# Graph network layer: the nodes' gates as tanh of the sums in PSUM, gated and added to the residual by three instructions per tile

## The chip, the cores and the metric

The kernel runs on one core of a Trainium2 chip. The time is the device time of one execution in microseconds (us), lower is better. Engines are named as in the profile: PE is TensorE, DVE is VectorE, ACT is ScalarE, POOL is GpSimd, and SP is the engine whose queue starts most transfers.

## The reference

One layer of a graph network with 12500 nodes and 400000 edges, the edges sorted by destination, all in float32, and then a residual and a layer norm. A node has 160 features: 64 scalars `s` and 32 vectors `v` of three components; `a` is the node's attribute. Cut to what matters:

```python
h_s = s @ lin1_ws * a / sqrt(64);  h_v = einsum('nci,cd->ndi', v, lin1_wv) * a / sqrt(32)
w1, w2, w3, w4, w5 = split(silu(edge_scalars @ fc_w1 / sqrt(64)) @ fc_w2 / sqrt(64))
es, ev = h_s[edge_src], h_v[edge_src]
mid_s, mid_v = products of w1..w5, es, ev and the four edge attributes
agg = segment_sum(mid, edge_dst) / 4
o_s = agg_s @ lin2_ws * a / sqrt(96);  o_v = agg_v @ lin2_wv * a / sqrt(128)
pre_s = s @ sc_ws * a / sqrt(64) + o_s          # 96 columns
pre_v = v @ sc_wv * a / sqrt(32) + o_v          # 32 x 3
scalars = silu(pre_s[:, :64]);  gates = sigmoid(pre_s[:, 64:96])
out = layernorm(x + concat(scalars, gates * pre_v))
```

Both `silu(z) = z * sigmoid(z)` and the gating of the vectors are a product with `sigmoid(z)` of the 96 columns of `pre_s`.

## The kernel before

**Start.** The table `h_tab` of 12500 rows of 160 numbers (`h_s`, `h_v`) is computed from the nodes and written to HBM; the destinations are turned into positions `rel` inside blocks of edges (L398, L403).

**The loop over edges.** 400000 edges are 3125 tiles of 128. A step takes four tiles; there are 782 steps. In a step:

- POOL issues four indirect transfers, `gather` (L452): each fetches the 128 rows of `h_tab` that a tile's sources name, into one of four buffers `hg`. POOL does nothing else in the loop.
- PE multiplies the hidden layer by `fc_w2` into `pw` (L465, PSUM, two buffers). The hidden layer itself comes every second step (`hidden`: PE L443, ACT silu L445).
- DVE makes the one-hot matrix of the destinations in a free part of `pw` (L528, from `rel` and `iota`, both in SBUF), the products of `pw` and `hg` (L475 and three times L483, one operand in PSUM and one in SBUF), and the selection matrix `sel` (L537, from the one-hot in PSUM).
- PE sums the products by destination into `pa` (L544), two steps later.

Every two blocks of three tiles, ACT copies `pa` to SBUF (L740), PE transposes it (L553), ACT copies that (L556, L558); for up to sixteen blocks together PE applies `lin2` (L568), ACT copies the result to `os` (L571), and DVE adds each block to the window of `acc` that begins at the block's first node (L576, all in SBUF). `acc` holds the sums of all nodes in SBUF, 96 rows (columns of `pre_s`, and of `pre_v`) by node. The self connection is added to it piece by piece (L720, L721).

**The nodes, inside the same loop.** When no later block can touch a group of four node tiles any more, `begin` takes up its job, one stage in each step (25 groups; `finish` issues the load of `xt`, the rows of x, at that moment in program order). In the stage `turn(k)`, one tile a step, PE transposes two 96 x 128 pieces of `acc` into a PSUM bank of the pool `misc` (two banks, shared with L443, L553, L568 and L720), and DVE multiplies by the attribute into `z`, in SBUF (L604). The multiplication stands between L475 and the first L483 of that step. The other stages stand at the end of a step, after `sel` and the additions to `acc`: `gates` (ACT sigmoid, L610), `gated` (DVE L615 and L616, two for each tile), `residual` (DVE L624, one for each tile), `moments` (L629, L631), `root` (ACT, L635) and `norm` (L639, L641, and the transfer to the output, L644). So a group of four takes ten steps. The last group of four tiles is done behind the loop; there each of L615, L616 and L624 takes all four tiles at once (`spans`).

**The order.** Within the loop the instructions of PE, DVE, ACT and POOL are issued in program order. The order of SP's queue, which starts the loads of `es`, `idx`, `eat`, `xt` and the output, is made by a planner. ACT loads a table (ACT_TABLE_LOAD) where a function is not in the table set that is loaded; the build places these.

Of the kernel before, what the change touches and what calls it, by code (L numbers as in the profile page):

```python
# [10 lines left out]
F32 = mybir.dt.float32  # L11
# [3 lines left out]
AF = mybir.ActivationFunctionType  # L15
OP = mybir.AluOpType
# [4 lines left out]
P = 128  # L21
S = 64
V = 32
V3 = 3 * V
D = S + V3
# [28 lines left out]
def gnn_kernel(  # L54
# [21 lines left out]
    nc = tc.nc  # L76
    N = x.shape[0]
    NT = attr.shape[1]
# [8 lines left out]
    consts = ctx.enter_context(tc.tile_pool(name="consts", bufs=1))  # L87
# [100 lines left out]
    def load_chunk(c, queue=nc.sync):  # L188
        if c in ess:
            return  # L190
        t0, halves = chunks[c]
        es = ess[c] = loads.tile([2 * S, SIDE * P], F32, name="es")
        for half, n in enumerate(halves):
            to = es[half * S:(half + 1) * S]
            e0 = (t0 + half * halves[0]) * P
            queue.dma_start(to[:, :n * P], es_t[:, e0:e0 + n * P])


    ident = consts.tile([P, P], F32, name="ident")
# [24 lines left out]
    with tc.tile_pool(name="nodes", bufs=len(starts)) as nodes, tc.tile_pool(  # L224
        name="nodes_ps", bufs=6, space=PSUM
# [22 lines left out]
        at = consts.tile([P, NT], F32, name="at")  # L248
# [60 lines left out]
        for c0, cn, quarters, cq, xa, xz in loaded:  # L309
# [3 lines left out]
            nt = -(-cn // P)  # L313
            first = c0 // P
            full = cn // P
            for t0 in range(0, nt, U):
# [5 lines left out]
                k = min(U, full - t0)  # L322
# [32 lines left out]

    load_chunk(0, nc.gpsimd)
    nc.gpsimd.dma_start(dt, dst)
    iota = consts.tile([P, W], F32, name="iota")
    nc.vector.tensor_copy(iota, iota_i)
    for half in range(2):  # L360
# [22 lines left out]
    for to, part, pieces, w, r0, c0, by in maps:  # L383
        for k, piece in enumerate(pieces):
# [3 lines left out]
            m = terms.setdefault((to, part, four), len(terms))  # L388
# [20 lines left out]
    acc = sums.tile([V3, 2, NP], F32, name="acc")  # L409
# [169 lines left out]
    def finish(fin, psum, t0, nt, p, most=NF):  # L579


        whole = nt if p == P else nt - 1
        spans = [(0, nt)] if t0 + nt == tiles_of_nodes else [(k, k + 1) for k in range(nt)]
        xt = fin.tile([P, most, D], F32, name="xt", bufs=2)
        held = []
        if whole < nt:
            nc.vector.memset(xt[:, whole], 0.0)
        parts = [(slice(t0 * P, (t0 + whole) * P), slice(0, whole), P)] if whole else []
        if whole < nt:
            parts.append((slice((t0 + whole) * P, (t0 + whole) * P + p), slice(whole, nt), p))  # L590
        for nodes_of, k, n in parts:
            nc.sync.dma_start(xt[:n, k], x[nodes_of, :].rearrange("(t p) d -> p t d", p=n))

        def turn(k):
            if not held:
                held.extend(fin.tile([P, most, *shape], F32, name=name) for name, shape in (
                    ("z", [2 * V3]), ("sg", [V3]), ("y", [D]), ("st", [6]), ("mv", [2]),
                    ("rs", [])))
            z = held[0]
            c = (t0 + k) * P  # L600
            pp = psum.tile([P, 2, V3], F32, name="pp", tag="misc")
            for m in range(2):
                nc.tensor.transpose(pp[:, m], acc[:, m, c:c + P], ident[:V3, :V3])  # L603
            return lambda: nc.vector.tensor_scalar(  # L604
                z[:, k], pp.rearrange("p m c -> p (m c)"), at[:, t0 + k:t0 + k + 1], None,
                op0=OP.mult)

        def gates():
            z, sg = held[:2]
            nc.scalar.activation(sg[:, :nt], z[:, :nt, :V3], AF.Sigmoid)  # L610

        def gated():
            z, sg, y = held[:3]
            for k, m in spans:
                nc.vector.tensor_mul(y[:, k:m, :S], z[:, k:m, :S], sg[:, k:m, :S])  # L615
                nc.vector.tensor_mul(  # L616
                    y[:, k:m, S:].rearrange("p t (c i) -> p t i c", i=3),
                    z[:, k:m, V3:].rearrange("p t (i c) -> p t i c", i=3),
                    sg[:, k:m, None, S:].to_broadcast([P, m - k, 3, V]))

        def residual():
            y = held[2]
            for k, m in spans:
                nc.vector.tensor_add(y[:, k:m], y[:, k:m], xt[:, k:m])  # L624

        def moments():
            _, _, y, st, mv, _ = held
            for k in range(nt):
                nc.vector.bn_stats(st[:, k], y[:, k])  # L629
            for k in range(nt):  # L630
                nc.vector.bn_aggr(mv[:, k], st[:, k])  # L631

        def root():
            mv, rs = held[4:]
            nc.scalar.activation(rs[:, :nt], mv[:, :nt, 1], AF.Sqrt, bias=eps)  # L635

        def norm():
            _, _, y, _, mv, rs = held
            nc.vector.reciprocal(rs[:, :nt], rs[:, :nt])  # L639
            for k in range(nt):  # L640
                nc.vector.tensor_scalar(y[:, k], y[:, k], mv[:, k, 0:1], rs[:, k:k + 1],  # L641
                                        op0=OP.subtract, op1=OP.mult)
            for nodes_of, k, n in parts:
                nc.sync.dma_start(out[nodes_of, :].rearrange("(t p) d -> p t d", p=n), y[:n, k])  # L644

        return [lambda k=k: turn(k) for k in range(nt)] + [
            gates, gated, residual, moments, root, norm]


    tiles_of_nodes = -(-N // P)  # L650
# [5 lines left out]
    with tc.tile_pool(  # L656
        name="fin", bufs=1
    ) as fin, tc.tile_pool(
        name="late", bufs=2
    ) as late, tc.tile_pool(name="edge", bufs=2) as edge, tc.tile_pool(  # L660
        name="deep", bufs=4
# [140 lines left out]
        def begin():  # L802

            if to_do and not turning and not doing:
                t, nt, p = to_do[0]
                end = (t + nt - 1) * P + p
                if not waiting or min(waiting) * RATE >= end + MARGIN:
                    job = finish(fin, misc_ps, *to_do.pop(0))
                    turning.extend(job[:nt])
                    doing.extend(job[nt:])  # L810

        with tc.manual_schedule(engines={ENG.PE, ENG.DVE, ENG.Activation, ENG.Pool}):
# [6 lines left out]
            for n, (c, i, tiles) in enumerate(steps):  # L819
# [36 lines left out]
                if n % 30 == 13 and pieces:  # L856
                    products_due.extend([lambda: (lambda: None)] * 3 + self_connection(pieces.pop(0)))
            assert not pieces and not products_due
            last_steps = finish(fin, misc_ps, *last_job, most=LAST)
            n = len(steps)  # L860
            while waits:
# [28 lines left out]
        with tc.For_i(0, n_redo, 1):  # L890
# [9 lines left out]
            with tc.For_i(0, n_again, 1) as g, tc.For_i(0, GT, 1) as k:  # L900
                t = g * GT + k
# [12 lines left out]
                for k, op in enumerate((OP.min, OP.max)):  # L914
# [14 lines left out]
                                        op1=OP.mult)  # L929
# [17 lines left out]
            for pool, job, most in [(fin, job, NF) for job in jobs] + [(fin, last_job, LAST)]:  # L947
                job_steps = finish(pool, misc_ps, *job, most=most)
                for f in job_steps[:job[1]]:
                    f()()  # L950
                for f in job_steps[job[1]:]:
                    f()
# [46 lines left out]
```

## Time and profile before

| | us |
|---|---|
| median of three runs | 4023.07 (4021.55 to 4029.47) |
| the profiled execution, its own time | 4018.78 |
| its span in the profile | 4017.0 |
| ACT's table loads at L445, L610, L635 | 61.6, 32.1, 32.1 (48, 25 and 25 of them) |
| ACT's activations at L610 | 12.6 and 0.4 (24 and 1) |
| idle time of PE before L603, of it for L604 | 90.7, 15.7 |

A line of a group in the profile reads: line, engine, operation, output <- inputs, shapes, count | busy us in all, mean ns of one | idle time of the engine before it, and what ended it. A line of the timeline reads: start, duration, engine, line, operation, count, and in brackets the idle time before it. Consecutive instructions of one line are merged there ("x4"), and the recorded ends of two instructions on DVE can overlap a little.

### The profile page before, as it was taken

The numbers are of one execution on the slowest core, as the hardware profiler recorded it, in microseconds if no ns is written. First come the engines' busy times: TensorE is split into PE (matmuls) and PEld (weight loads), VectorE is DVE, ScalarE is ACT, GpSimd is POOL, SyncE is SP. The second block draws the span as 40 slices with busy tenths as digits, with TensorE's granted clock in tenths as the row PEclk, the third lists the DMA queues.
The fourth block names the chain that finished last, engine by engine and source line by source line (L and its number), as shares of the span: only waits on it lengthen the run. The fifth ranks groups of instructions, "written<-read, shape, count | busy, mean of one in ns | idle before, by whom it ended". The sixth has DMA issues, their size and how long they took to land. (4 is left out here: it accounts for less than half of the span.)

```text
span 4017.0 us, 46675 instructions
## 1 busy us (share of the span) xinstructions
PE 3676.3 (92%) x14291; PEld 1588.0 (40%) x14291; DVE 2410.5 (60%) x6596; ACT 938.7 (23%) x2463; POOL 2982.9 (74%) x3144
## 2 busy tenths in 40 slices
PE   6899899999999999999999999999899989999997
PEld 4344343343343433334333443344343334333443
DVE  5556565655655655656656655666565665655655
ACT  2222222221222222212212222222121221222222
POOL 4777777777777777777777777777777777777775
PEclk8999999999999999999999999999999999999999
DMA  8444444443444444444444444444444444444442
GB/s 240 95 100 98 98 104 96 103 106 94 101 102 98 103 98 102 103 100 101 101 99 100 95 106 101 96 106 99 98 105 95 105 102 95 103 101 98 100 96 58
DMA packets 227691, 411.71 MB, mean 102 GB/s; under 512 B 71883, under 2 KB 157383, under 8 KB 226535
## 3 DMA queue, kind: packets, MB, share of 16 engines
q0 software_dynamic: 152272, 266.53, 27.9%
q1 hardware_dynamic: 74646, 142.01, 14.7%
q8 instruction: 115, 1.88, 0.2%
q14 instruction: 144, 1.18, 0.1%
q10 hardware_dynamic: 514, 0.10, 0.0%
HBM read 392.41 MB, written 16.00 MB: 102 GB/s over the span
## 5 line engine op out<-in xcount | busy, mean ns | idle before, releaser
L452 POOL DMA_INDIRECT hg<-h_tab,idx x3125 | 2968.7, 950 | 962.2 <-issue 865.5
L465 PE MATMUL pw<-w,hid 128*128 128x448 f32 x3126 | 1376.5, 564 | 191.5 <-DVE sel L537 150.1
L544 PE MATMUL pa<-pr,sel 128*64 128x416 f32 x6250 | 1303.5, 539 | 0.0
L475 DVE TENSOR_TENSOR pr<-pw,hg 128x512 f32<-128x512 f32 x782 | 540.5, 691 | 1042.4 <-DMA hg<-h_tab,idx 784.2
L483 DVE TENSOR_TENSOR pr<-pw,hg 128x384 f32<-128x384 f32 x2346 | 1153.6, 547 | 0.0
L465 PEld LDWEIGHTS pw<-w,hid 128*128 128x128 f32 x3126 | 556.3, 195 | 685.8 <-issue 445.3
L544 PEld LDWEIGHTS pa<-pr,sel 128*64 128x64 f32 x6250 | 388.0, 139 | 812.3 <-issue 799.4
L740 ACT COPY sa<-pa 128x416 f32<-128x416 f32 x521 | 263.1, 505 | 1415.4 <-PE pa L544 1413.0
L443 PE MATMUL misc<-es,w 128*128 128x512 f32 (+1 forms) x784 | 448.0, 654 | 17.0 <-DMA es<-in_es_t_dram 14.3
L528 DVE TENSOR_TENSOR pw<-rel,iota 128x64 f32<-128x64 int16 x782 | 178.4, 228 | 468.3 <-PE pw L465 465.5
L445 ACT ACTIVATE hid<-misc 128x512 f32<-128x512 f32 x392 | 233.5, 596 | 743.9 <-PE misc L443 743.4
L553 PEld LDWEIGHTS misc<-ident,sa 128*128 128x128 f32 x2084 | 239.6, 141 | 311.6 <-issue 252.1
L568 PE MATMUL misc<-tt,l 128*96 128x256 f32 (+5 forms) x1496 | 346.0, 378 | 1.7 <-ACT tt L558 1.5
L553 PE MATMUL misc<-ident,sa 128*128 128x128 f32 x2084 | 328.1, 280 | 0.9 <-DVE acc L721 0.8
L537 DVE TENSOR_TENSOR sel<-pw,eas 128x256 f32<-128x256 f32 x782 | 323.6, 414 | 0.0
L556 ACT COPY tt<-misc 128x192 f32<-128x192 f32 x521 | 164.5, 316 | 517.2 <-PE misc L553 516.7
L568 PEld LDWEIGHTS misc<-tt,l 128*96 128x96 f32 (+1 forms) x1496 | 227.0, 162 | 139.6 <-issue 72.6
L443 PEld LDWEIGHTS misc<-es,w 128*128 128x128 f32 x784 | 119.2, 191 | 283.2 <-issue 228.5
L576 DVE TENSOR_TENSOR acc<-acc,os 96x32 f32 x1042 | 195.6, 188 | 23.9 <-ACT os L571 5.5
L603 PE MATMUL misc<-ident,acc 96*128 96x96 f32 x196 | 36.4, 272 | 90.7 <-DVE pw L528 41.8
L558 ACT COPY tt<-misc 128x64 f32<-128x64 f32 x521 | 117.1, 225 | 0.0
L571 ACT COPY os<-misc 96x512 f32<-96x512 f32 (+2 forms) x68 | 38.3, 563 | 303.1 <-PE misc L568 280.4
(84 smaller groups left out, 653.0 us busy)
## 6 DMA issues: line engine op xcount, KB each, us to landing
es<-in_es_t_dram SPq DMA_DIRECT2D x258, 384.0 KB
hg<-h_tab,idx POOLq DMA_INDIRECT x3125
h_tab<-ht POOLq DMA_DIRECT2D x6, 1280.0 KB
xt<-in_x_dram SPq DMA_DIRECT2D x23, 320.0 KB
out_dram<-y SPq DMA_DIRECT2D x23, 320.0 KB
xv<-in_xv_t_dram SPq DMA_DIRECT2D x25, 187.5 KB
xs<-in_xs_t_dram SPq DMA_DIRECT2D x25, 125.0 KB
xa<-in_xs_t_dram SPq DMA_DIRECT2D x6, 512.0 KB
```

The lines of the kernel that those rows point to most:

```text
L443: nc.tensor.matmul(ph[:k, c], w1[:k, :k], es[:k, t0 * P + c0 * P:t0 * P + c1 * P], start=True, stop=True)
L445: nc.scalar.activation(hid[:k, c], ph[:k, c], AF.Silu, scale=1.0 / math.sqrt(64))
L452: nc.gpsimd.indirect_dma_start(out=hg[:, t, :], out_offset=None, in_=h_tab, in_offset=bass.IndirectOffsetOnAxis(ap=i, axis=0))
L465: nc.tensor.matmul(pw[:, t:t + m, :NWT], hid[:m * S, c * P:(c + 1) * P], w2[:m * S, :m], start=True, stop=True)
L475: nc.vector.tensor_mul(two, pw[:, :n, :2 * S].rearrange("p t (k c) -> p t k c", k=2), hg[:, :n, None, :S].to_broadcast([P, n, 2, S]))
L483: nc.vector.tensor_mul(pr[:, :n, first:first + V3].rearrange("p t (i c) -> p t i c", i=3), pw[:, :n, None, 2 * S + k * V:2 * S + (k + 1) * ...
L537: nc.vector.tensor_mul(sel[:, :n], oh[:, :, None, :].to_broadcast([P, n, 4, W]), by_slot(tiles[0][0])[:, u:u + n, :, None].to_broadcast([P ...
L544: nc.tensor.matmul(pa[half * ROWS:(half + 1) * ROWS, :NPR], sel[:, t].rearrange("p k w -> p (k w)"), pr, start=start, stop=stop)
L553: nc.tensor.transpose(pt[:, four * P:four * P + k], sa[:k, c:c + P], ident[:k, :k])
L568: nc.tensor.matmul(po[:, k, :nb], l2[r, terms[to, part, four]], a[:, :nb], start=(n == 0), stop=(n == len(of) - 1))
L576: nc.vector.tensor_add(window, window, os[:, :, b])
L740: nc.scalar.copy(sa, pas.pop(j)[:, :NPR])
```

## The change

The gate is written with `sigmoid(a*p) = (1 + tanh(a*p/2)) / 2`, p being the sums before the multiplication by the attribute. `half_at` is half of the attribute, made once ahead of the loop. In `turn(k)` ACT takes the tanh straight from the PSUM bank, with `half_at` as its scale, into `g` in SBUF. Then DVE, at the place where L604 stood, issues three instructions for the tile: `(g + 1) * p` for the scalars and for the vectors, both read from and written to the same PSUM bank, and `that * half_at + xt` into `y`. The stages `gates`, `gated` and `residual`, the tile `z`, and the batching of the last group fall away; a group of four takes seven steps.

```diff
+    half_at = consts.tile([P, NT], F32, name="half_at")
+    nc.vector.tensor_scalar_mul(half_at, at, 0.5)
...
-        spans = [(0, nt)] if t0 + nt == tiles_of_nodes else [(k, k + 1) for k in range(nt)]
...
-            z = held[0]
+            g, y = held[:2]
             c = (t0 + k) * P
-            pp = psum.tile([P, 2, V3], F32, name="pp", tag="misc")
+            pp = psum.tile([P, 512], F32, name="pp", tag="misc")
             for m in range(2):
-                nc.tensor.transpose(pp[:, m], acc[:, m, c:c + P], ident[:V3, :V3])
-            return lambda: nc.vector.tensor_scalar(
-                z[:, k], pp.rearrange("p m c -> p (m c)"), at[:, t0 + k:t0 + k + 1], None,
-                op0=OP.mult)
-
-        def gates():
-            z, sg = held[:2]
-            nc.scalar.activation(sg[:, :nt], z[:, :nt, :V3], AF.Sigmoid)
-
-        def gated():
-            z, sg, y = held[:3]
-            for k, m in spans:
-                nc.vector.tensor_mul(y[:, k:m, :S], z[:, k:m, :S], sg[:, k:m, :S])
-                nc.vector.tensor_mul(
-                    y[:, k:m, S:].rearrange("p t (c i) -> p t i c", i=3),
-                    z[:, k:m, V3:].rearrange("p t (i c) -> p t i c", i=3),
-                    sg[:, k:m, None, S:].to_broadcast([P, m - k, 3, V]))
-
-        def residual():
-            y = held[2]
-            for k, m in spans:
-                nc.vector.tensor_add(y[:, k:m], y[:, k:m], xt[:, k:m])
+                nc.tensor.transpose(pp[:, m * V3:(m + 1) * V3], acc[:, m, c:c + P], ident[:V3, :V3])
+            half = half_at[:, t0 + k:t0 + k + 1]
+            nc.scalar.activation(g[:, k], pp[:, :V3], AF.Tanh, scale=half)
+            pg = pp[:, 2 * V3:2 * V3 + D]
+
+            def gate():
+                nc.vector.scalar_tensor_tensor(pg[:, :S], g[:, k, :S], 1.0, pp[:, :S],
+                                               op0=OP.add, op1=OP.mult)
+                nc.vector.scalar_tensor_tensor(
+                    pg[:, S:].rearrange("p (c i) -> p i c", i=3),
+                    g[:, k, None, S:].to_broadcast([P, 3, V]), 1.0,
+                    pp[:, V3:2 * V3].rearrange("p (i c) -> p i c", i=3),
+                    op0=OP.add, op1=OP.mult)
+                nc.vector.scalar_tensor_tensor(y[:, k], pg, half, xt[:, k],
+                                               op0=OP.mult, op1=OP.add)
+
+            return gate
...
         return [lambda k=k: turn(k) for k in range(nt)] + [
-            gates, gated, residual, moments, root, norm]
+            moments, root, norm]
```

More of the change, by code (lines that the diff above doesn't have):

```diff
@@ L596, in turn @@
                 held.extend(fin.tile([P, most, *shape], F32, name=name) for name, shape in (
-                    ("z", [2 * V3]), ("sg", [V3]), ("y", [D]), ("st", [6]), ("mv", [2]),
-                    ("rs", [])))
-            z = held[0]
+                    ("g", [V3]), ("y", [D]), ("st", [6]), ("mv", [2]), ("rs", [])))
+            g, y = held[:2]
             c = (t0 + k) * P
-            pp = psum.tile([P, 2, V3], F32, name="pp", tag="misc")
+            pp = psum.tile([P, 512], F32, name="pp", tag="misc")
@@ L626, in moments @@
+            return gate
         def moments():
-            _, _, y, st, mv, _ = held
+            _, y, st, mv, _ = held
             for k in range(nt):
@@ L633, in root @@
         def root():
-            mv, rs = held[4:]
+            mv, rs = held[3:]
             nc.scalar.activation(rs[:, :nt], mv[:, :nt, 1], AF.Sqrt, bias=eps)
         def norm():
-            _, _, y, _, mv, rs = held
+            _, y, _, mv, rs = held
             nc.vector.reciprocal(rs[:, :nt], rs[:, :nt])
```

## The prediction

> **What bounds the kernel now.** I began with the page's busy times.
>
> ```profile
> span 4017.0 us, 46675 instructions
> PE 3676.3 (92%) x14291; PEld 1588.0 (40%) x14291; DVE 2410.5 (60%) x6596; ACT 938.7 (23%) x2463; POOL 2982.9 (74%) x3144
> ```
>
> TensorE looks like the bound, GpSimd does not. So I asked next, of each engine, what it waited for. This is GpSimd's answer (total us, times, longest):
>
> ```profile
> POOL hg L452 <- issue: 865.5, 2841, 0.3
> POOL hg L452 <- DVE pw L528: 22.8, 75, 0.3
> POOL hg L452 <- DMA h_tab<-ht: 10.5, 1, 10.5
> ```
>
> After the first gather, no wait of GpSimd is longer than 0.3 us, whatever is named: that is the fixed gap between two gathers. The view of the gathers' tile has their durations:
>
> ```profile
> L452 POOL DMA_INDIRECT hg<-h_tab,idx x3125: 942/946/2035, 65.4 to 3984.9; - x196
> ```
>
> A gather (0.946) and its gap (0.30) make 1.250 us, and 3124 x 1.25 = 3905.0 of the 3919.4 us between first and last start. The loop is one unbroken chain of gathers on GpSimd, and its length is 3905.0 plus what single gathers lose. TensorE and VectorE follow it: VectorE waits 784.2 us in all for gathered rows. They would hold it up only by freeing one of the four hg buffers late. From the last product of a step (L483) to the first gather that reuses its buffer there were 11.0 us in the median, 4.8 at the least (step 4), 5.7 after step 30. No delay below that can reach the end.
>
> So the question is what makes single gathers slow: 14.4 us in all. I laid GpSimd's timeline beside VectorE's. GpSimd around the second longest gather:
>
> ```profile
> 2463.54 0.94 POOL L452 DMA_INDIRECT hg<-h_tab,idx  x1 [0.30 <-issue]
> 2464.79 1.97 POOL L452 DMA_INDIRECT hg<-h_tab,idx  x1 [0.30 <-issue]
> 2467.07 0.95 POOL L452 DMA_INDIRECT hg<-h_tab,idx  x1 [0.30 <-issue]
> ```
>
> VectorE at that moment:
>
> ```profile
> 2464.47 0.40 DVE L576 TENSOR_TENSOR acc<-acc,os 96x32 f32 x2
> 2464.79 1.02 DVE L624 TENSOR_TENSOR y<-y,xt 128x160 f32<-128x160 f32 x4
> 2465.73 0.22 DVE L528 TENSOR_TENSOR pw<-rel,iota 128x64 f32<-128x64 int16 x1
> ```
>
> The gather starts as the four residual additions start and ends 1.02 us late: exactly their length. Going through all 3125 starts, the time above 1.250 sums to 5.5 us over the 47 intervals in which the gating products L615 or L616 ran, 5.6 us over the 45 with L624, 1.0 over 5 at the start (L398, L403), 0.9 over 548 with the additions L576, 0.5 over 442 with the one-hot L528, and 0.1 over the 1958 intervals beside all else, L475, L483, L537 and L604 among them. (The missing 0.6 is 3124 x 0.0002, the median's own fraction.) The dividing line is where the operands are: L615, L616, L624, L576, L528 and L398 read two tensors from SBUF. L483 and L537 read one from PSUM and one from SBUF, and cost the gathers nothing. When a run of the first kind covers a gather's start, the gather ends later by about what is left of that run.
>
> **The change, part by part.** The rows that price it:
>
> ```profile
> L483 DVE TENSOR_TENSOR pr<-pw,hg 128x384 f32<-128x384 f32 x2346 | 1153.6, 547 | 0.0
> L604 DVE TENSOR_SCALAR z<-misc,at 128x192 f32<-128x192 f32 x98 | 39.8, 408 | 0.4 <-PE misc L603 0.4
> L641 DVE TENSOR_SCALAR y<-y,mv,rs 128x160 f32<-128x160 f32 x98 | 30.7, 373 | 0.9
> L616 DVE TENSOR_TENSOR y<-z,sg 128x96 f32<-128x96 f32 (+1 forms) x95 | 27.2, 286 | 0.0
> L624 DVE TENSOR_TENSOR y<-y,xt 128x160 f32<-128x160 f32 (+1 forms) x95 | 24.9, 321 | 0.0
> L615 DVE TENSOR_TENSOR y<-z,sg 128x64 f32<-128x64 f32 (+1 forms) x95 | 20.6, 217 | 0.6 <-ACT sg L610 0.6
> ```
>
> Removed on VectorE: 39.8 + 27.2 + 24.9 + 20.6 = 112.5 us. Added: 98 times three scalar_tensor_tensor, a form the trace lacks. At 1.04 ns an element, L483 is 400 + 147 ns, L641 167 + 206 with pointer scalars. So I estimate 64 elements at 0.22, 96 at 0.26 and 160 with a pointer at 0.37 us: 0.85 a tile, 83 us. VectorE's 29 us less lie beside the gathers and are worth nothing by themselves. On ScalarE 25 sigmoids (12.6 + 0.4) go, with the 25 table loads at L610 (32.1) and some 25 reloads for silu. 98 tanh come: the sigmoid takes 523 ns for 384 elements and 364 for 192, so 0.28 for 96. That too is beside the gathers.
>
> The trace shows no tanh. The built program's order puts no table load before a tanh in the loop; sqrt keeps its pair. The Trainium skill (ScalarE: Activation LUTs, Table sets: the hidden batching unit) speaks against mixing functions, lists tanh with exp and with sigmoid, and silu nowhere in that table. By it each turning step would pay a load for tanh and one for silu, and with the 1283 ns that a load takes here VectorE would start a gate 1.3 us later: still inside the 5.7, so the sum would be the same.
>
> What acts on the chain: the 11.2 us (5.5 + 5.6, unrounded 11.16) lost to L615, L616 and L624 go, if the new three cost the gathers nothing. The first two read g from SBUF and the sums from PSUM, the third PSUM, xt and a pointer. Bounds: nothing, by the 1958 intervals; or what two SBUF operands cost. For that I laid a run of 0.82 us from each start of z (L604) over the gathers' starts: it covers 75 and sums to 32.3 us. I take nothing: L483 has the same places of operands as the third, L604 a pointer, and both are in the free group. The Trainium skill (GPSIMD Engine Reference, Key points) names VectorE instructions with two SBUF inputs, as seen here, but also those in a 2-port mode; were L641, SBUF to SBUF with one tensor, such a one, it would be a loss that this change leaves in place. The 46 intervals beside L641 lost 0.1 us.
>
> What moves: in a turning step the gate occupies VectorE for some 0.82 us where z took 0.32 (start to start), so the additions and the next one-hot come 0.5 us later against the gathers. Only 41 turning steps have such additions. Shifting them in the trace by 0.35 to 0.65 us makes them cover 7 to 18 starts, 0.3 to 0.7 us. I take +0.6; bounds -0.9 (all that L576 costs now) to 41 x 0.12 (its largest single loss) = +4.9.
>
> New waits. A gate waits for its tanh, and L483 and the selection queue behind it on VectorE. ScalarE is 23% busy and what stands before the tanh is matched to earlier matmuls, so this is a fraction of a microsecond against 5.7. The PSUM bank of the turned sums is held about 0.5 us longer; TensorE waited 15.7 us for z, may wait some 50 more, and has 340 us of idle time. Three steps fewer per group end the job earlier. SP's queue: xt needs the buffer of two groups before, and is issued when that group's residual ends (2465.83, behind the L624 above), a whole group ahead of its use, so reading it at the first turn waits for nothing; in the built order xt moves ahead of one pair of es loads, whose buffer comes free eight steps of 5.0 us before use. half_at is one instruction of 0.2 us before the gathers.
>
> The tail, from the last sums to the statistics:
>
> ```profile
> 4001.06 0.63 DVE L641 TENSOR_SCALAR y<-y,mv,rs 128x160 f32<-128x160 f32 x2
> 4001.63 0.74 DVE L604 TENSOR_SCALAR z<-misc,at 128x192 f32<-128x192 f32 x2
> 4002.72 0.74 DVE L604 TENSOR_SCALAR z<-misc,at 128x192 f32<-128x192 f32 x2 [0.35 <-PE misc L603]
> 4005.09 0.82 DVE L624 TENSOR_TENSOR y<-y,xt 128x640 f32<-128x640 f32 x1
> 4005.95 1.01 DVE L629 BATCH_NORM_STATS2 st<-y 128x6 f32<-128x160 f32 x4
> ```
>
> The group before ends in the loop after the change, so its L641 is gone here. First pair turned by 4001.5, tanh 4001.8, then four gates of 0.82 to 0.90 us, the third behind its bank: 4005.3 where L629 began at 4005.95. I take -0.65; bounds -2 to +1.
>
> Sum: 4018.78 - 11.2 + 0.6 - 0.65 = 4007.5 by the profiled execution. That one is 4.3 us under the median of the runs (4023.07; 4021.55 to 4029.47), so the same step gives 4011.8. Part of that scatter may itself be such losses and would go too: 4011.5.
>
> **The rivals.**
> Losses move (17%): the later additions and one-hots land on starts much oftener than the shift says. For: each gather start is a target every 1.25 us. Against: 41 steps, at most 0.12 us each in the trace. Price 4.9, or 11.8 if all 98 tiles paid: 4016 to 4023.
> The chain does not react (7%): the long gathers have another cause in those steps, such as SP's xt transfer. For: it is issued in the same step. Against: at 2464.79 the gather is already running when xt goes out. Only the tail is left: 4022.4.
> Slower (8%): the three PSUM instructions hold GpSimd off as two SBUF operands do. Place: the gate run in each turning step; price 32.3 - 11.2 - 0.65 = +20.4, so 4043.5. It decides from 11.85 / 98 = 0.12 us per tile. Against: L483 and L604.
>
> **How the numbers follow.** The forecast has 68%. 0.2% (8.05 us, about what a measurement of this kernel can tell) is passed in most of it: 0.65 faster, with a little of the first rival. Within: 0.27. Slower: 0.08. The range: 4005 (bounds -0.9 and -2, and no offset between profile and median) to 4022, which takes in +4.9 and +1 with the offset and most of the rivals within 0.2%; the slow rival is left out.
>
> **What would show it.** Right: no gather interval above 1.4 us in the node steps, first to last gather start some 10.5 us under 3919.4, and L629 at the end 20.5 us after the last gather's start (21.1 now). Wrong: gathers still long where VectorE runs the gate; a GpSimd wait over 0.3 us (a buffer freed late); table loads beside tanh; VectorE waiting for xt.

## The result and the profile after

| | before | after |
|---|---|---|
| median us (runs, lowest to highest) | 4024.39 (10, 4019.44 to 4033.12) | 4014.72 (10, 4006.09 to 4017.3) |
| after / before | | 0.9971, 95% interval 0.9963 to 0.998 |
| the profiled execution, its own time | 4018.78 | 4006.09 |
| first to last gather start, from the timeline | 3919.43 | 3909.84 |
| of it above 3124 x 1.250 | 14.4 | 4.8 |

The change makes the kernel 9.7 us faster: 0.24%, by the interval 0.2 to 0.37%. From the page of the profile after, GpSimd's waits and the view of the gathers' tile, these are the lines that stand against those of before:

```profile
span 4004.3 us, 46674 instructions
PE 3666.2 (92%) x14291; PEld 1586.3 (40%) x14291; DVE 2407.4 (60%) x6508; ACT 897.4 (22%) x2488; POOL 2973.4 (74%) x3144
...
POOL hg L454 <- issue: 848.3, 2785, 0.3
...
POOL hg L454 <- DMA h_tab<-ht: 6.6, 1, 6.6
...
L454 POOL DMA_INDIRECT hg<-h_tab,idx x3125: 942/946/1278, 61.3 to 3971.1; - x196
```

The gathers' median is 946 ns as before, the longest 1278 ns where it was 2035 (after: L454, at the start of the loop; before: L452). VectorE is busy for 3 us less and ScalarE for 41 less; both lie beside the chain of gathers, which accounts for the time. The two profiled executions differ by 12.7 us, and the differences come from three places:

- The chain of gathers, 9.6 us: 3919.43 - 3909.84.
- The first gather, 4.15 us: it starts at 61.27 where it was 65.42, since GpSimd waited 6.6 us for the last write of the table and not 10.5. That is not the change's doing. In the other profiles on chips of this speed it started between 61.7 and 64.4 us. It may be one source of the runs' scatter.
- The end, -1.0 us: from the last gather's start to the end of the span it takes 33.2 us where it took 32.15.

The chain's 9.6 us are also what the medians moved by (9.67); that the two agree to 0.1 us is chance, since the medians' own interval is 8.0 to 14.9 us. The timeline shows a gate with a gather in it, VectorE and GpSimd together:

```profile
2287.47 0.23 DVE L609 SCALAR_TENSOR_TENSOR misc<-g,misc 128x64 f32<-128x64 f32 x1
2287.73 0.26 DVE L611 SCALAR_TENSOR_TENSOR misc<-g,misc 128x96 f32<-128x96 f32 x1
2288.03 0.38 DVE L616 SCALAR_TENSOR_TENSOR y<-misc,half_at,xt 128x160 f32<-128x160 f32 x1
2288.15 0.94 POOL L454 DMA_INDIRECT hg<-h_tab,idx  x1 [0.30 <-issue]
```

The gather starts 0.12 us into the addition of xt and takes 0.94 us, the normal time. Over all 169 intervals in which L609, L611 or L616 ran, the time above 1.250 sums to -0.02 us, and none is over 0.03. What is left of the loss is 2.5 us beside the additions (now L578), 0.7 beside the one-hot (now L530), 1.0 at the start (L400, L405) and 0.3 in the 51 intervals with L636, the last multiplication of a tile (L641 before, where it was 0.1 in 46).

### The profile page after: what moved, and what is told of

Read it like the earlier page. It is cut to its first block, busy times and chain, and to the rows that moved or that the text cites. A ratio compares the mean times of both kernels' runs of the same rounds, so it can differ in the third digit from the quotient of the medians.

```text
span 4004.3 us, 46674 instructions
## 1 busy us (share of the span) xinstructions
PE 3666.2 (92%) x14291; PEld 1586.3 (40%) x14291; DVE 2407.4 (60%) x6508; ACT 897.4 (22%) x2488; POOL 2973.4 (74%) x3144
## 5 line engine op out<-in xcount | busy, mean ns | idle before, releaser
L454 POOL DMA_INDIRECT hg<-h_tab,idx x3125 | 2959.2, 947 | 958.2 <-issue 848.3
L485 DVE TENSOR_TENSOR pr<-pw,hg 128x384 f32<-128x384 f32 x2346 | 1152.6, 546 | 0.0
L530 DVE TENSOR_TENSOR pw<-rel,iota 128x64 f32<-128x64 int16 x782 | 178.6, 228 | 500.6 <-PE pw L467 498.8
L578 DVE TENSOR_TENSOR acc<-acc,os 96x32 f32 x1042 | 195.2, 187 | 25.2 <-ACT os L573 6.9
```

Of the source, the lines that this page charges most:

```text
L454: nc.gpsimd.indirect_dma_start(out=hg[:, t, :], out_offset=None, in_=h_tab, in_offset=bass.IndirectOffsetOnAxis(ap=i, axis=0))
L485: nc.vector.tensor_mul(pr[:, :n, first:first + V3].rearrange("p t (i c) -> p t i c", i=3), pw[:, :n, None, 2 * S + k * V:2 * S + (k + 1) * ...
L578: nc.vector.tensor_add(window, window, os[:, :, b])
```

## The experiments

The theory: GpSimd's gather is delayed when it starts while VectorE reads two tensors from SBUF, and the change helps because its three instructions read one of them from PSUM. The rivals: it helps because four tiles' instructions in a row became one tile's three at a time; or because sigmoid and its table loads went; or the losses had another cause in those steps.

The first four ran on a chip on which the kernel before took 4019.69 us (median of 28) and GpSimd's chain was the bound as in the profile of before. "Loss" is the time above 1.250 us between two gather starts, put down to the VectorE line that ran in that interval.

**All operands in SBUF, the instructions where the change has them.** ScalarE copies the sums to SBUF and the intermediate stays in SBUF; the rest is the changed kernel:

```diff
+            nc.scalar.copy(zs[:, k], pp[:, :2 * V3])
-            pg = pp[:, 2 * V3:2 * V3 + D]
+            pg = us[:, k]
...
-                ... g[:, k, :S], 1.0, pp[:, :S] ...
+                ... g[:, k, :S], 1.0, zs[:, k, :S] ...
-                    pp[:, V3:2 * V3].rearrange("p (i c) -> p i c", i=3),
+                    zs[:, k, V3:].rearrange("p (i c) -> p i c", i=3),
```

> The changed kernel with the same stages, places and instruction counts on VectorE, but the gate's operands in SBUF: ScalarE copies the turned sums to SBUF behind the tanh, and the three scalar_tensor_tensor read and write SBUF only. Theory (two SBUF operands hold the gathers off): laying a run of 0.85 us from each first gate instruction of the changed kernel's trace over its gather starts covers 70 starts and sums to 30.5 us; a gather may slip in between two of the three, so 10 to 30 us are lost there: the chain of gathers 3920 to 3940 us instead of 3909.8, and a time 10 to 30 us over the changed kernel's. Rival (the dense burst of eight or four instructions in one step is what hurts, and the change spread it over four steps): no loss, 3909 to 3911, the changed kernel's time.

Measured: 4007.97 us, ratio to before 0.9971 (0.9959 to 0.9982); chain 3915.75. The gate's lines (L612, L614, L619) lost 1.36 us in 169 intervals, the longest 0.14. The theory asked for 10 to 30 us: its size was wrong by about a factor of ten. The timeline shows why:

```profile
3258.40 0.21 DVE L612 SCALAR_TENSOR_TENSOR us<-g,zs 128x64 f32<-128x64 f32 x1
3258.53 0.28 DVE L614 SCALAR_TENSOR_TENSOR us<-g,zs 128x96 f32<-128x96 f32 x1
3258.85 0.38 DVE L619 SCALAR_TENSOR_TENSOR y<-us,half_at,xt 128x160 f32<-128x160 f32 x1
3258.97 1.08 POOL L454 DMA_INDIRECT hg<-h_tab,idx  x1 [0.30 <-issue]
```

The same phase as in the example above, 0.12 us into the addition of xt, and with both operands in SBUF the gather is 0.14 us late. So the place of the operands does decide. But the delay ends 0.26 us after that instruction's start (starts at 0.17 and 0.22 lose 0.09 and 0.04), and the gathers that start 0.13 to 0.39 us after the start of L614 lose 0.01 us at most: they get through before L619, which waits for L614's result. The gate is not one run of 0.82 us but short ones with openings, and little is lost even from SBUF. This run's other 9.4 us of loss lie beside the additions (2.65), the one-hot (1.36), the start (1.2), and 4.2 over all other intervals. Of the 4.2, 0.52 is a single wait of GpSimd for L485 (0.82 us in the place of 0.30, at 3547 us). Most of the rest is no delay of single gathers: all through this run the undisturbed gathers took 1 to 3 ns longer (median 947 ns, many at 949), which makes some 3 us in these intervals. Why is open. The profiled execution was the longest of the kernel's seven (4012.13 us), so its chain need not be that of the median.

**The addition of xt alone reading two tensors from SBUF.**

```diff
-            pg = pp[:, 2 * V3:2 * V3 + D]
+            pg = us[:, k]
```

> The changed kernel, only the product of the first two gate instructions written to SBUF instead of PSUM, so that the third reads two tensors from SBUF and the first two still one from PSUM. Theory: only the third holds gathers off; a run of 0.2 to 0.28 us from its places in the changed kernel's trace covers 12 to 14 starts and sums to 1.8 to 2.9 us: chain 3911 to 3913. Rival (dense burst): 3909 to 3911. Either is within 0.2% of the changed kernel; the gathers that start during the third instruction tell them apart.

Measured: 4010.94 us, 0.9976 (0.9967 to 0.9985); chain 3910.88. The addition (L618 there) lost 0.83 us over 118 intervals, the longest 0.14, with the same phases: starts 0.12 to 0.18 us into it lose 0.14 to 0.09. By its size alone the chain would fit the rival as well; it is the phases that tell for the theory, since in the changed kernel starts at the same places lose nothing (0.83 us in all was lost where the theory had 1.8 to 2.9).

**The old stages, with tanh.** The kernel before with its stages, buffers and places, `half_at` and tanh in the place of sigmoid, `(g + 1) * z` in the place of `z * sg`:

```diff
-            nc.scalar.activation(sg[:, :nt], z[:, :nt, :V3], AF.Sigmoid)
+            nc.scalar.activation(sg[:, :nt], z[:, :nt, :V3], AF.Tanh)
...
-                nc.vector.tensor_mul(y[:, k:m, :S], z[:, k:m, :S], sg[:, k:m, :S])
+                nc.vector.scalar_tensor_tensor(y[:, k:m, :S], sg[:, k:m, :S], 1.0, z[:, k:m, :S],
+                                               op0=OP.add, op1=OP.mult)
```

> The kernel before with one part of the change alone: tanh in place of the sigmoid (half of the attribute in the first multiplication, and 1 + tanh in the two gating products), all in SBUF and in the old stages. Some 50 of ScalarE's 98 table loads go. Theory: time as before within 0.2%, gathers still lose 8 to 14 us beside the gating products and the residual. Rival (the table loads or the tanh brought the gain): the changed kernel's time, about 0.3% below.

Measured: 4016.99 us, 0.9997 (0.9988 to 1.0006); chain 3919.56. ScalarE is busy for 876.1 us where it was 938.7, with the table loads beside the gate gone but one, and the losses are what they were: 5.1 us at the gating, 6.0 at the residual. Tanh and fewer table loads bring nothing by themselves. In the changed kernel, tanh has no load beside it either.

**The additions ahead of the selection.** After the change, half of the remaining loss lies beside the additions L578. Here they stand before `sel`, whose first operand is in PSUM, so that they are no longer followed by the next step's one-hot:

```diff
-                sel = select_quad(edge, tiles, oh)
                 for a in ready:
                     add(*a)
+                sel = select_quad(edge, tiles, oh)
```

> The changed kernel with the additions to the nodes' sums moved ahead of the selection matrix, so that they no longer end where the next one-hot begins (both read two tensors from SBUF). Theory: the 2.5 us lost beside additions in the changed kernel fall to 0.5 to 2, as a run of 0.4 us that no longer joins the one-hot; chain 3908 to 3910, time the same within 0.2%. If additions lose more at their new phase, up to 41 x 0.2 = 8 us more.

Measured: 4008.86 us, 0.9973 (0.9964 to 0.9982); chain 3910.63. The loss did not go, it changed its name: 0.55 us beside the additions (the longest 0.03) and 2.24 beside the one-hot (the longest 0.15). So it is the one-hot (228 ns), and not the additions (187 ns each), that delays gathers here, though both read two tensors from SBUF. The changed kernel's timeline shows it, once one looks for it:

```profile
1820.08 0.41 DVE L578 TENSOR_TENSOR acc<-acc,os 96x32 f32 x2
1820.35 1.09 POOL L454 DMA_INDIRECT hg<-h_tab,idx  x1 [0.30 <-issue]
1820.40 0.22 DVE L530 TENSOR_TENSOR pw<-rel,iota 128x64 f32<-128x64 int16 x1
```

The gather starts late in the additions, the one-hot 0.05 us after the gather, and the gather is 0.14 us late. A VectorE instruction can still delay a gather that has started just before it.

**The operands' place by itself.** The other kernels ran on chips where the kernel before took 5089 to 5189 us: there, with a granted clock of 0.87 to 0.88 where it was 0.97, GpSimd waits for VectorE, so the time of a kernel says little about the gathers and the gathers' own durations are compared. What sets this is open. GpSimd's largest wait in the first of these kernels:

```profile
POOL hg L454 <- DVE pr L485: 1020.8, 229, 11.9
```

The measure is the duration of a gather above 0.946 us, summed over those gathers in whose first 0.3 us the line in question ran. By it, the gates and residuals of the kernel before lose 5.52 us (28 gathers) + 5.62 (24) = 11.1 us, as by the starts. Sums of this measure are taken from the trace's nanoseconds; the timeline's two decimals are too coarse for sums over hundreds of gathers.

Three kernels add one VectorE instruction of 128 x 320 elements to every step of the changed kernel, its result unused: the sum of two SBUF tensors, the sum of one tensor in PSUM and one in SBUF, and one SBUF tensor times a constant.

```diff
+                sc = edge.tile([P, Q, 80], F32, name="sc")
+                nc.vector.tensor_add(sc[:, :m], one, two)               # both in SBUF
+                nc.vector.tensor_add(sc[:, :m], pw[:, :m, :80], two)    # or: one in PSUM
+                nc.vector.tensor_scalar_mul(sc[:, :m], one, 2.0)        # or: one tensor, in SBUF
```

> The changed kernel with one more addition on VectorE at the end of each of the 782 steps, 128 x 320, both operands in SBUF, into a scratch tile that nobody reads. Theory: laying a run of 0.35 us at that place over the gather starts of the changed kernel covers 176 starts and sums to 34 us, some more where the next one-hot joins it: time 25 to 70 us over the changed kernel's. Rival (VectorE's busy time, whatever the operands): the same as with one operand in PSUM.

> The same extra addition at the same place, one operand in PSUM (the step's own pw) and one in SBUF. Theory: 0 to 4 us over the changed kernel, though VectorE has 782 x 0.48 = 375 us more to do: the gathers' chain does not see it. Rival (VectorE's busy time): as with two SBUF operands.

> The same place and size, a multiplication by a constant with its one tensor in SBUF. By the trace of before, where 46 gather intervals beside L641 lost 0.1 us, 0 to 4 us over the changed kernel. By the rule of the Trainium skill (GPSIMD Engine Reference, Key points) that an instruction in a 2-port mode contends as well, a loss like that with two SBUF operands, shorter by the time the mode saves: 10 to 40 us.

The first two were run again on another chip:

> The changed kernel with one more addition on VectorE at the end of each of the 782 steps, 128 x 320, both operands in SBUF. On the chip where it ran first the kernel before itself took 5089 us and GpSimd waited for VectorE, so the times said nothing; the gathers' own busy time was 53 us above that with one operand in PSUM. On a chip where the gathers are the chain: 30 to 70 us over the changed kernel's time. Rival (VectorE's busy time, whatever the operands): the same as with one operand in PSUM.

> The same extra addition, one operand in PSUM: 0 to 4 us over the changed kernel, though VectorE has 374 us more to do. Rival: as with two SBUF operands.

| the added instruction | its mean ns | gathers beside it | they lose, us | longest | ratio of times (95%) |
|---|---|---|---|---|---|
| SBUF + SBUF | 489 | 461 | 52.1 | 0.56 | 1.0013 (0.9981 to 1.0046) |
| again | | 447 | 48.2 | 0.54 | 0.9948 (0.9916 to 0.998) |
| PSUM + SBUF | 478 | 446 | -0.24 | 0.03 | 1.0103 (1.0072 to 1.0134) |
| again | | 449 | 0.05 | 0.13 | 1.0032 (0.9998 to 1.0066) |
| one SBUF tensor | 334 | 358 | 11.2 | 0.24 | 1.0018 (0.9983 to 1.0052) |

The pair differs in the place of one operand, and with it the loss comes and goes, some 110 ns for each gather against nothing. Two thirds of it lie in the 137 gathers that also had the additions L578 just ahead of the added one (34 of the 52 us); with the operand in PSUM the 133 gathers at that place lose nothing. What was expected of the times could not be read there, and no run shows this loss in a kernel's time: the kernel with no delayed gathers was even the slower of the two. One example from the timeline of each, SBUF and SBUF:

```profile
116.19 0.48 DVE L844 TENSOR_TENSOR sc<-w,l 128x320 f32<-128x320 f32 x1
116.27 1.23 POOL L454 DMA_INDIRECT hg<-h_tab,idx  x1 [0.30 <-issue]
```

PSUM and SBUF:

```profile
226.24 0.48 DVE L844 TENSOR_TENSOR sc<-pw,l 128x320 f32<-128x320 f32 x1
226.31 0.95 POOL L454 DMA_INDIRECT hg<-h_tab,idx  x1 [0.30 <-issue]
```

One SBUF tensor:

```profile
2998.16 0.32 DVE L844 TENSOR_SCALAR sc<-w 128x320 f32<-128x320 f32 x1
2998.24 1.05 POOL L454 DMA_INDIRECT hg<-h_tab,idx  x1 [0.30 <-issue]
```

Each gather starts 0.07 or 0.08 us into the instruction; they take 0.28, 0.00 and 0.10 us longer than 0.946. The third is the surprise: one SBUF tensor is enough in this form. It is not the one-hot that follows: 282 of the 358 gathers have none beside them, and these lose 7.9 us of the 11.2. (About 1 us of the 11.2 is no delay: in this run the median gather takes 949 ns and not 946.) So of the two expectations the trace's 0 to 4 us failed, and the skill's 10 to 40 us held, at its lower edge and in gather time. In the first kernel, the gathers with no one-hot near lose 0.27 us in the mean where they start 0.05 to 0.15 us into the addition, 0.14 at 0.2, 0.065 at 0.3 and nothing from 0.35 on: the delay ends some 0.14 us before the instruction's recorded end.

**The old bursts, one operand of each in PSUM.** The counterpart of the first experiment: stages, order and bursts of the kernel before, but the gating and the residual read columns of `pw` in the place of the gate and of `y`. The gate and the gated sums are so left out of what is computed.

```diff
-                nc.vector.tensor_mul(y[:, k:m, :S], z[:, k:m, :S], sg[:, k:m, :S])
+                nc.vector.tensor_mul(y[:, k:m, :S], z[:, k:m, :S], now["pw"][:, k:m, :S])
...
-                nc.vector.tensor_add(y[:, k:m], y[:, k:m], xt[:, k:m])
+                nc.vector.tensor_add(y[:, k:m], now["pw"][:, k:m, :D], xt[:, k:m])
```

> The kernel before with its stages and bursts as they were (eight gating products, then four additions, back to back at the end of a step), but the sigmoid operand of the products, and y in the residual, replaced by columns of the step's own pw in PSUM: the gate and the first operand of the residual are left out of the computation. All twelve instructions then read one tensor from PSUM. Theory (a run of instructions with two SBUF operands holds a gather until the run ends): the 11.2 us go although the bursts stay; chain 3908 to 3911 us, time about 0.25 to 0.3% below the kernel before. Rival (the burst itself hurts, which would explain why the gate in SBUF at one tile a step lost only some 1.4 us): the chain stays at 3918 to 3921 and the time as before.

Measured: 5185.29 us where before took 5176.7 there, 1.0009 (0.9986 to 1.0032); the expected chain and time could not be read on this chip, where GpSimd waits 1182.8 us for L483. The 31 gathers beside the gating lose 0.00 us and the 23 beside the residual 0.03, in the place of 5.52 (28 gathers) and 5.62 (24). In the timeline a gather starts in the middle of the four residual additions and is not late:

```profile
915.66 1.01 DVE L626 TENSOR_TENSOR y<-pw,xt 128x160 f32<-128x160 f32 x4
915.92 0.94 POOL L452 DMA_INDIRECT hg<-h_tab,idx  x1 [0.30 <-issue]
```

With it the four corners are filled, in us of gather time lost at the gates and residuals, by durations:

| | both operands in SBUF | one in PSUM |
|---|---|---|
| in bursts of up to four tiles | 11.1 (before) | 0.0 |
| a tile at a time | 1.1 (all in SBUF) | 0.0 (after) |

Either half of the change alone takes away nine tenths of the loss or more. Both theory and first rival hold, and each was incomplete: for a loss of this size it takes two reads from SBUF *and* a run without an opening.

**The one-hot's second operand in PSUM.** The row of counting numbers that the one-hot is compared with is put into spare columns of `pw`'s two buffers ahead of the loop:

```diff
-                                iota[:, None, :].to_broadcast([P, n, W]), op=OP.is_equal)
+                                pw[:, :n, NWT + W:], op=OP.is_equal)
```

> The changed kernel with the counting row of the one-hot kept in spare PSUM columns of the two pw tiles, so that the one-hot reads one tensor from SBUF and one from PSUM. Theory: what is left of the gathers' losses in the loop (0.7 us beside the one-hot and 2.5 beside additions, most of which end where a one-hot begins) falls to 0 to 1.5: chain 3906 to 3909, time 1 to 4 us below the changed kernel's, which its measurement can hardly tell. Rival (the additions are what costs there): chain unchanged at 3909 to 3911, the gathers still long where an addition ends beside a one-hot.

> The changed kernel with the one-hot's counting row in spare PSUM columns, once more, for its time: where it ran first the kernel before itself took 5089 us. There the gathers beside a one-hot or an addition ended 1.0 us late in all, where the changed kernel has 4.2. Theory, on a chip where the gathers are the chain: first to last start 3906 to 3908 us (the changed kernel 3909.8), time 1 to 4 us under the changed kernel's 0.9971 of the kernel before, so a ratio of 0.996 to 0.997. Rival (nothing left to gain): 3909 to 3911 and 0.997.

Measured: 5097.34 us where before took 5088.63 (1.0012, 0.9985 to 1.0039), and again 5177.1 against 5188.69 (0.9984, 0.9954 to 1.0014). The gathers beside the one-hot and the additions lose 0.9 and 0.8 us by the measure, none more than 0.03, where in the changed kernel they lose 3.2 (the 4.2 of the expectation, and its 1.0, were summed from durations rounded to 0.01 us). On these chips the gathers lie differently, so the fair comparison is with the two runs above that had the added instruction with one operand in PSUM, and the one-hot in SBUF: of their 49 and 51 gathers that start between 0.06 us before a one-hot and 0.075 us after its start, 11 and 16 were late by over 0.02 us. Here it is none of 51 and 69. So it is the one-hot's second read from SBUF that delays them.

A gain does not follow from that. In both runs the median gather takes 949 ns where it took 946, and all gathers together 2963.8 and 2963.4 us where the changed kernel has 2959.2: that costs more than the delays did. The kernel with one SBUF tensor has the 949 too; the kernels with two SBUF operands and with one in PSUM, run on the same chip as it and the first of these, do not. What lengthens every gather of a kernel by 3 ns is open, and the time of this kernel on a chip where the gathers are the bound was not measured.

## Why the prediction was right, and where not

**The chain as the bound: right.** The median moved by 9.67 us and the chain by 9.59, while VectorE's busy time fell by 3. The forecast was 11.6 under the median shown of before, and the two mis-sized terms below are 2.9 us of the difference in the profile's sum; in the medians 1.9 us of it can be seen, which is within their interval (8.0 to 14.9 us faster). That the profiled execution took 4006.09 us where the sum said 4007.5 is luck: the 2.9 us that the two terms missed were made up by the first gather, which started 4.15 us earlier for no reason of the change.

**The 11.2 us: right,** in mechanism and in size. They went in whole (-0.02 left), no interval in the node steps is above 1.4 us, and the corners above show that the place of operands is a sufficient cause. The choice between the two bounds, by the nearest rows (L483, and L604 with its pointer), held. One reading behind it did not: that the second longest gather was late by "exactly" the length of the four additions. The one-hot that follows begins before the additions' recorded end and belongs to the run: all 15 gathers that were late by over 0.1 us beside L624 with a one-hot behind it were held until 0.08 to 0.09 us into that one-hot.

**The price of the slower rival, 32.3 us: wrong by more than ten times.** It took the gate as one run of 0.82 us in which a gather waits to the end. The kernel with all operands in SBUF is that rival made real: 1.36 us lost by starts, and it is faster than the kernel before, with a ratio no worse than that of the change itself. So the choice of the operands, with the gate at its new place, decided about 1 us and not 32. The prediction's rule, that a gather ends later by "about what is left of that run", was read from L624, whose four additions do not depend on each other and start before the recorded end of the one ahead (four of 321 ns in 1.02 us). The gate's last instruction waits for the one before, and the gather slips in there.

**The +0.6 for what moves: mis-sized, +1.8.** The additions and the one-hot lost 1.4 us and lose 3.2 (by durations 1.3 and 3.2; the other three profiles on a chip of this speed give 2.6 to 2.9 by durations for kernels with the gate in the same place). The prediction priced the additions as they cover starts. The runs show that the one-hot delays the gather, also when it begins just after the gather has started, which a count of covered starts leaves out. Of the first rival ("losses move") this is the right half; the 4.9 us that it asked were not reached.

**The tail, -0.65: wrong, +1.0.** The timeline of the end, all engines:

```profile
3989.21 0.38 DVE L616 SCALAR_TENSOR_TENSOR y<-misc,half_at,xt 128x160 f32<-128x160 f32 x1
...
3989.74 0.55 PE L603 MATMUL misc<-ident,acc 96*128 96x96 f32 x2 [1.18 <-DVE misc L609]
...
3990.34 0.34 ACT L605 ACTIVATE g<-misc,half_at 128x96 f32<-128x96 f32 x1 [1.40 <-PE misc L603]
...
3990.71 0.23 DVE L609 SCALAR_TENSOR_TENSOR misc<-g,misc 128x64 f32<-128x64 f32 x1 [0.26 <-ACT g L605]
...
3992.42 0.99 DVE L624 BATCH_NORM_STATS2 st<-y 128x6 f32<-128x160 f32 x4
```

The third tile's transposes wait for the bank that the first tile's gate (L616, to 3989.59) frees (the line names L609, which ended last before them; the fourth tile's transposes start 0.14 us behind L616 in the same way); transposes (0.55), tanh (0.34) and gate then follow one another, and VectorE has a hole between the second tile's gate and 3990.71. The prediction said "behind its bank" but gave the four gates 0.82 to 0.90 us each, with no hole, and the tanh 0.28. From the end of the additions to the statistics it takes 4.8 us where it took 5.0. The additions themselves end 0.4 us later after the last gather, so the statistics begin 21.3 us after its start (forecast 20.5, before 21.1), and the last output transfer is longer by 0.8.

**What was said of the rest: right, but for VectorE's busy time.** No wait of GpSimd in the loop is over 0.3 us; no table load stands beside tanh; VectorE doesn't wait for xt; TensorE waits 21.8 us for L616 where it waited 15.9 for z (some 50 more were allowed). The three instructions take 220, 262 and 384 ns (0.22, 0.26 and 0.37 were estimated). VectorE's busy time was to fall by 29 us and fell by 3: the sum of the durations did fall by 28 (112.5 to 84.8), but the old instructions overlapped in the record, and the page counts an overlap once. As the prediction said, nothing hung on it.

**The one-tensor case: the row was too weak.** L641, one tensor from SBUF to SBUF, was taken as harmless from 46 intervals that lost 0.1 us. The single-tensor kernel lost 11.2 us. Here the Trainium skill (GPSIMD Engine Reference, Key points) names both kinds, two SBUF inputs and a 2-port mode, and the runs agree with it: the third added instruction handled its 320 elements in 334 ns where the sum of two tensors took 489, as a mode of that kind would; the mode itself is inferred. L641 does the same on a small scale. Most of its 0.1 us was one gather, 0.075 us late, that started in the middle of four L641 in a row, and the changed kernel shows two more, where nothing else ran (L636 there):

```profile
2314.03 1.18 DVE L636 TENSOR_SCALAR y<-y,mv,rs 128x160 f32<-128x160 f32 x4
2314.47 1.01 POOL L454 DMA_INDIRECT hg<-h_tab,idx  x1 [0.30 <-issue]
```

That was the loss which, as the prediction put it, the change would leave in place: 0.1 us in 46 intervals before, 0.3 in 51 after. A small sum over 46 intervals did not mean that the form is harmless; few gathers had started at the place that counts.

The 4.3 us between the profiled execution and the median, taken over from before, were 8.6 here: the profiled execution of the changed kernel is the fastest of its ten.

## What to carry to other kernels

Where GpSimd issues indirect gathers in an unbroken chain, a VectorE instruction that reads two tensors from SBUF may delay one, and so may one that reads and writes a single tensor in SBUF; what counts is the length of the uninterrupted run. Here it was enough to put one operand in PSUM, or to break the run into pieces of which one waits for the other. An engine that is 60% busy and on nobody's chain of waits can so still lengthen the bound, and no wait names it: look for it in the longest durations of the bounding engine, against the timeline of the other. And price such a cover from the instructions' dependences, not from first start to last end.

## What the runs showed of the hardware

- Alone, an instruction with two SBUF operands delayed a gather by at most 0.02 us at 187 ns (the additions), 0.14 at 384 ns and 0.32 at 489 ns; a gather that started 0.35 us into the last was not delayed at all. In runs of independent instructions the delay reached 1.09 us (gating products) and 1.02 us (four additions and the one-hot behind them). Three gathers of the kernel before got through between two instructions of such a run (0.10, 0.11 and 0.17 us late).
- The Trainium skill (SBUF — State Buffer, Who interferes with whom) says of the 2-port modes that the one who comes first has the shared pair for the whole instruction; of the two-input case here the hold is shorter than the recorded instruction by some 0.12 to 0.14 us, and in a run of independent instructions it mostly lasts across them.
- The gathers hardly delay VectorE: the added addition took 489 ns with both operands in SBUF and 478 with one in PSUM, in kernels where 461 and 446 gathers lay beside it.
- A one-hot that begins 0.03 to 0.06 us after a gather still delays it by up to 0.15 us.
- The tanh of 96 columns from PSUM, with a pointer as scale, takes 340 ns, and no table load lies between it and silu in the loop.
- In some kernels the median gather takes 949 ns in the place of 946, in one of them in two runs on two chips. What sets that is open.
